# A 12-layer decoder on one core: the causal mask moves from TensorE to a fused VectorE operation, and three small steps change engine

## The chip, the core and the metric

The kernel runs on one core of a Trainium2 chip. The metric is the device time of one execution in microseconds. Before the change it is 2720.16 us (median of three runs, 2719.19 to 2727.39).

## What is computed

The reference is a post-norm decoder of twelve layers, four rounds of self-mixing, cross-attention and feed-forward, each as `x = layernorm(x + layer(x))`, on `x` of 4 x 512 x 128 (batches, positions, width) with a context of 4 x 154 x 128. Four of the layers bear on this case.

```python
# L0_xattn: cross-attention whose result goes through a residual and a norm of its own
# L1_ffn (8 heads of 64, gated experts) and L2_attn (16 heads of 64, keys = values): causal
sim  = einsum('bhid,bhjd->bhij', q * scale, k)
sim  = where(causal_mask, very_negative, sim)
attn = softmax(sim, axis=-1)
out  = einsum('bhij,bhjk->bhik', attn, values)
# L2_xattn: cross-attention with biases on q, k, v
q = einsum('bsd,ed->bse', query, Wq) + bq
```

## The kernel before, in words

Everything stays on chip between layers. The program gives each engine one list of instructions in the order in which the Python code issues them; a tile framework adds the semaphore waits. So the order of the code is the order on every engine's queue, and an engine that waits holds up all that stands behind it on its own queue. Layers overlap at their seams: an outer loop calls the generators of two layers in turn, after patterns written by hand (`ORDER`, `BESIDE`), and during one layer it also issues weight loads and `send` calls for the next.

**The causal layers.** A unit is two heads (one per half of the partitions) of one batch: 16 units in `l1_ffn`, 32 in `l2_attn`. The class `Causal` cuts a unit's score triangle into three parts, A, B and C (`PARTS`): A is query tile 3 with 512 keys, B is query tile 2 with 384 keys and tile 0 with 128, C is tile 1 with 256. Each part has the two heads in the two banks of one PSUM tile `scc`. For each part:

- `scores` (L1124): matmuls q x k into `scc` (L1131), and then a bf16 matmul of the identity with a 128 x 128 triangle of -2^100 or 0, `cmaskb`, that accumulates the mask onto the diagonal block (L1137), two per query tile: 8 per unit.
- `maxima` (L1147): one VectorE reduction per query tile for both heads, PSUM to `nm`, with the sign turned (L1149): 4 per unit.
- `exps` (L1151): ScalarE exp of the score plus `nm`, PSUM to `pr`, with the row sum in `zs` (L1155): 8 per unit.
- `norm` (L1160): VectorE reciprocal of `zs` (L1161), GpSimd multiplies `pr` by it (L1164).
- `turned` (L1170): TensorE transposes of `pr` into PSUM `ptc` (L1180), copied to `pT`; `products` (L1188): matmuls with the values into `avc` (L1193).

In `l2_attn.step` (L1506) part A's copy to `pT` is on VectorE (L1516), B's on ScalarE (L1527), C's on VectorE (L1541). The step handles unit i+1's scores beside unit i's transposes and products, and makes unit i+2's queries and keys (`psqk`, L1465; `q` on VectorE L1469, `k` on ScalarE L1470) and values (`psv`, L1475; L1478). Its output projection is `ypo` (L1486). All these PSUM tiles share three places of two banks each, so a matmul that opens a tile waits until the tile that had the place was read. `l1_ffn.step` (L1352) has the same three parts among more TensorE work (`psve` L1283, `psg` L1305, `yT` L1326) and more VectorE work (`vtmp` L1288, `gT` L1310).

**send** (L396) prepares queries or keys of the next attention: a projection in PSUM, ScalarE adds the bias and scales (`raw`, L408; a bias scaled first on VectorE, L406), GpSimd splits `raw` in three bf16 parts (L409 to L412), and SP writes them out. Queries are 512 columns wide, keys 154. Seven of the eight sends of L2_xattn fall into the L2_attn stage.

**L0_xattn** is `cross_attention` with `shuffled=True`: 16 units of four heads. A step (L1037) has two halves, each with two score tiles, two VectorE reductions to `top` (L963) and exps. Between the halves `link_maxima` (L493) brings the maxima of the next unit into the queries: TensorE transposes `pmx` (L499), then a VectorE add to `qP` (L501). At the end of a step GpSimd splits the maxima in four small operations (L488 to L491). In `more_sums` (L996) a unit's result is transposed on VectorE (`ot`, L1012), a reciprocal is taken (L1014), and GpSimd multiplies (`zt`, L1015). After the last unit of a batch `inner` adds the residual on GpSimd and takes statistics on VectorE; `outer` (L1029) subtracts the mean and scales, four operations by `applied` on GpSimd (L346), then three GpSimd operations with gamma, beta and the residual (L1031 to L1033).

Of the kernel before, what the change touches and what calls it, by code (L numbers as in the profile page):

```python
# [11 lines left out]
F32 = mybir.dt.float32  # L12
BF16 = mybir.dt.bfloat16
U8 = mybir.dt.uint8
I32 = mybir.dt.int32
AF = mybir.ActivationFunctionType
ALU = mybir.AluOpType
AX = mybir.AxisListType
# [3 lines left out]
P = 128  # L22
B, S, D = 4, 512, 128
NT = S // P
H, DK = 16, 8
KC = 154
# [3 lines left out]
MASKED = -float(2**100)  # L30
# [144 lines left out]
def decoder_kernel(ctx: ExitStack, tc: tile.TileContext, x, ctxT, mask1, mask3, packs, offsets, out, layers):  # L175
# [168 lines left out]
    def applied(dst, ys, n, mv, rs, on=nc.vector):  # L344
        for t in range(n):
            on.tensor_scalar(  # L346
                dst[:, t, :], ys[:, t, :], mv[:, t, 0:1], rs[:, t : t + 1], ALU.subtract, ALU.mult
            )
# [44 lines left out]
    Q_ROWS, K_ROWS = ((1, 1, 3), (6, 1, 2), (0, 1, 1)), ((0, 3, 3), (1, 6, 2), (2, 1, 1))  # L393
    SLOT = 32

    def send(far, order, w, rhs, scale, bias, raw, part, on=nc.gpsimd, by=nc.sync):  # L396

        n = rhs.shape[-1]
        pj = psum_t("ps_proj", kind="a" if "a" in ring else "t")
        nc.tensor.matmul(pj[:, :n], lhsT=w, rhs=rhs, start=True, stop=True)  # L400
        if bias is None:
            nc.scalar.activation(raw, pj[:, :n], AF.Copy, scale=scale)
        else:
            if scale != 1.0:
                scaled_bias = small.tile([P, 1], F32, tag="sb", name="sb", bufs=2)
                nc.vector.tensor_scalar(scaled_bias, bias, scale, None, ALU.mult)  # L406
                bias = scaled_bias
            nc.scalar.activation(raw, pj[:, :n], AF.Identity, bias=bias, scale=scale)  # L408
        on.tensor_copy(part[:, 0, :], raw)  # L409
        on.tensor_tensor(raw, raw, part[:, 0, :], ALU.subtract)  # L410
        on.tensor_copy(part[:, 1, :], raw)
        on.tensor_tensor(part[:, 2, :], raw, part[:, 1, :], ALU.subtract)  # L412
        for i, (at, gap, m) in enumerate(order):
            for r in range(2):
                rows = far[r].rearrange("(s k) p c -> (k p) s c", k=DK)
                by.dma_start(
                    rows[:, at : at + gap * (m - 1) + 1 : gap, :],
                    part[64 * r : 64 * r + 64, i : i + 1, :].to_broadcast([64, m, n]),
                )
# [7 lines left out]
    def sends(i, x_T):  # L427

        name, w = layers[i], weights[layers[i]]
        if name.endswith("xattn"):  # L430
            scale = 1.0 if name == "L0_xattn" else DK ** -0.5

            def key(b):
                return lambda room: send(
                    far_kc[b], K_ROWS, w["wk"], ctx_sb[:, b, :], 1.0, w.get("bk"), *room(KC)
                )

            def query(b):
                return lambda room: send(
                    far_q[i % 2][b], Q_ROWS, w["wq"], x_T[:, b, :], scale, w.get("bq"), *room(S)  # L440
                )

            return [x for b in range(B) for x in ((-1, ("k", b), key(b)), (b, ("q", b), query(b)))]
        if name == "L3_attn":
            xd = []

            def down(room):
                xd.append(room("xd"))
                pd = psum_t("xd", kind="a" if "a" in ring else "t")
                nc.tensor.matmul(pd, lhsT=w["wd"], rhs=x_T[:, 0, :], start=True, stop=True)  # L450
                evacuate(xd[0], pd)

            scale = DK ** -0.25
            return [
                (0, "down", down),
                (0, ("q", 0), lambda room: send(far_q[i % 2][0], Q_ROWS, w["wq"], xd[0], scale, None, *room(S))),
                (0, ("k", 0), lambda room: send(far_k[0], K_ROWS, w["wk"], xd[0], scale, None, *room(S))),
            ]
        return []
# [356 lines left out]
    def cross_attention(w, cur, new, last, room, scale, mask=None, shuffled=False):  # L816
# [179 lines left out]
        def more_sums(n):  # L996
            b, j = divmod(n, 4)
            m = made[b]
            av = m["av"]
            nc.tensor.matmul(  # L1000
                av, lhsT=m["v2"][:, j].rearrange("p g k -> p (g k)"), rhs=weights_of.pop((n, 4)),
                start=False, stop=True, skip_group_check=True,
            )
            if not shuffled:
                avs = copied(av, keep)
                agenda.add(n + 2, [lambda: divided(avs, m["o"], j)])
                if j == 3:
                    agenda.add(n + 3, out_pieces(b, m["o"], w, keep, cur, new, last, split=True))
                return

            ot = keep.tile([P, 16, 32], F32, tag="ot", name="ot", bufs=2)
            nc.vector.transpose(ot.rearrange("p s k -> p (s k)"), av.rearrange("p (q s) -> p s q", s=16))  # L1012
            rec = small.tile([P, 16], F32, tag="recx", name="recx")
            nc.vector.reciprocal(rec, ot[:, :, DK])  # L1014
            nc.gpsimd.tensor_tensor(  # L1015
                m["zt"][:, j, :].rearrange("p (s d) -> p s d", d=DK), ot[:, :, :DK],
                rec[:, :, None].to_broadcast([P, 16, DK]), ALU.mult,
            )
            if j == 3:
                zt = m["zt"]  # L1020
                xs = cur["x"][:, b * NT : (b + 1) * NT, :]
                ys = keep.tile([P, NT, D], F32, tag="ys", name="ys")
                stats = []

                def inner():
                    nc.gpsimd.tensor_tensor(zt, zt, xs, ALU.add)
                    stats.extend(ln_stats(zt, NT, "i"))

                def outer():  # L1029
                    applied(ys, zt, NT, *stats, on=nc.gpsimd)  # L1030
                    nc.gpsimd.tensor_tensor(ys, ys, w["gamma"][:, None, :].to_broadcast([P, NT, D]), ALU.mult)  # L1031
                    nc.gpsimd.tensor_tensor(ys, ys, w["beta"][:, None, :].to_broadcast([P, NT, D]), ALU.add)
                    nc.gpsimd.tensor_tensor(ys, ys, xs, ALU.add)  # L1033

                agenda.add(n + 2, [inner, outer] + finish_pieces(b, ys, new, last, split=True))
# [72 lines left out]
    class Causal:  # L1108
# [6 lines left out]

        def __init__(self, pool, room):
            self.ap, self.room, self.work = pool, room, None
            self.mask = pool.tile([P, P], BF16, name="cmaskb", bufs=1)
            make_causal_mask(nc, self.mask, MASKED)
            self.nm = {}  # L1120
            self.pr = {}
            self.pT = {}

        def scores(self, u, part, q, k):  # L1124

            sc = psum2("scc")
            for i, (qt, at) in enumerate(self.PARTS[part]):
                n = (qt + 1) * P
                for r in range(2):
                    rows = slice(64 * r, 64 * r + 64)  # L1130
                    nc.tensor.matmul(  # L1131
                        sc[:, r, at : at + n], lhsT=q[rows, qt * P : n], rhs=k[rows, :n], start=(i == 0), stop=False,
                        skip_group_check=True,
                    )
            for qt, at in self.PARTS[part]:
                for r in range(2):
                    nc.tensor.matmul(  # L1137
                        sc[:, r, at + qt * P : at + (qt + 1) * P], lhsT=identb, rhs=self.mask, start=False, stop=True,
                        skip_group_check=True,
                    )  # L1140
            nt = len(self.PARTS[part])
# [3 lines left out]
            self.pr[u, part] = pr  # L1145

            def maxima():  # L1147
                for i, (qt, at) in enumerate(self.PARTS[part]):
                    nc.vector.tensor_reduce(nm[:, i, :], sc[:, :, at : at + (qt + 1) * P], AX.X, ALU.max, negate=True)  # L1149

            def exps():  # L1151
                for i, (qt, at) in enumerate(self.PARTS[part]):
                    to = at + (qt + 1) * P
                    for r in range(2):
                        nc.scalar.activation(  # L1155
                            pr[:, r, at:to], sc[:, r, at:to], AF.Exp, bias=nm[:, i, r : r + 1],
                            accum_out=zs[:, i, r : r + 1],
                        )

# [39 lines left out]
    def l1_ffn(w, cur, new, last, room):  # L1199
# [19 lines left out]
        def gate(b):  # L1219
# [20 lines left out]

            def split():
                rest = gm.rearrange("p (t c r) e -> p t c (r e)", t=NT, c=NC)
                left = pool.tile([P, NT, NC, 2 * NE], F32, tag="left", name="left", bufs=1)
                for i in range(3):
                    part = pb[:, :, :, i, :]
                    nc.gpsimd.tensor_copy(part, rest)
                    if i < 2:
                        nc.gpsimd.tensor_tensor(left, rest, part, ALU.subtract)
                        rest = left
# [1156 lines left out]
```

## Time and profile before

| | |
|---|---|
| profiled execution, own time | 2720.02 us |
| its span on the core | 2718.2 us |
| median of the runs | 2720.16 us |
| granted TensorE clock, mean | 0.954 |
| busy share TensorE, VectorE, ScalarE, GpSimd | 90%, 62%, 46%, 39% |
| L0_xattn, 4 x 4 units | about 249 to 393 us |
| L1_ffn | about 985 to 1440 us |
| L2_attn | about 1446 to 1860 us |
| mask matmuls L1137 | 384 |
| reductions L1149 | 192, 820 ns mean |
| reciprocal and multiply of L0_xattn, L1014 and L1015 | 16 each, 253 and 406 ns |

How to read what follows. A row of a timeline is start (us), duration (us), engine, line, operation, output <- inputs, shapes, and after `x` how many instructions in a row are merged; in brackets the idle time before it and what ended it. A row of the chain of waits is start, length and what the chain passes through; the chain is followed back from the last instruction of the program, so what lies on it sets the end. TensorE rows are pipelined: the start of the next row tells more than the end of one. PEld is TensorE's weight load.

### The profile page before, as it was taken

To read this page: it belongs to the slowest core of one execution; us is meant where nothing else is said; L and a number is where in the kernel's file an instruction comes from. 1 tells how busy PE (TensorE), PEld (TensorE's weight loads), DVE (VectorE), ACT (ScalarE), POOL (GpSimd) and SP (SyncE) were. 2 spreads that over 40 slices of the span, in tenths; PEclk is the share of its full clock that TensorE was granted. 3 is DMA by queue.
4 is the path that set the end of the run, shared out by engine and by line. 5 is a ranking of instruction groups with operands and counts; after the bars stand their busy time and mean duration, and the time that the engine had idled before them with its cause. 6 is when DMAs were issued, how large, how long until landed. Compare 5 with 4: busy or idle time off the path is not lost. (4 is left out here: it accounts for less than half of the span.)

```text
span 2718.2 us, 38015 instructions
## 1 busy us (share of the span) xinstructions
PE 2445.7 (90%) x14378; PEld 1179.3 (43%) x14378; DVE 1681.6 (62%) x2872; ACT 1251.3 (46%) x2533; POOL 1071.5 (39%) x1406
## 2 busy tenths in 40 slices
PE   5898789988877989999999999998988999899998
PEld 1233234433333444444444555554455233445665
DVE  6796741188997665555445555556755887664444
ACT  3775432377652433333233555553543777343221
POOL 2342540157675326555452444443355342320000
PEclk7998989989989999999999999998997899899999
DMA  5421310000002400000000000002102240410000
GB/s 153 116 79 57 100 35 0 1 0 1 0 16 75 146 7 1 1 1 1 1 1 1 15 10 3 12 13 72 49 1 59 71 120 20 132 33 1 5 5 8
DMA packets 75559, 96.40 MB, mean 35 GB/s; under 512 B 23664, under 2 KB 62320, under 8 KB 75376
## 3 DMA queue, kind: packets, MB, share of 16 engines
q1 hardware_dynamic: 74224, 92.14, 11.7%
q8 instruction: 113, 1.85, 0.3%
q10 hardware_dynamic: 1152, 1.84, 0.2%
q14 instruction: 70, 0.57, 0.1%
HBM read 63.92 MB, written 33.49 MB: 36 GB/s over the span
## 5 line engine op out<-in xcount | busy, mean ns | idle before, releaser
L1164 POOL TENSOR_TENSOR pr<-pr,zs 128x1024 f32<-128x1024 f32 x192 | 237.1, 1252 | 234.2 <-DVE zs L1161 185.4
L670 DVE TENSOR_REDUCE top<-sc 128x2 f32<-128x1024 f32 x256 | 300.8, 1215 | 46.1 <-PE sc L666 43.2
L691 ACT ACTIVATE pT<-st 128x512 f32<-128x512 f32 x512 | 276.2, 598 | 88.2 <-PE st L682 85.1
L1155 ACT ACTIVATE pr<-scc,nm 128x256 f32<-128x256 f32 (+3 forms) x384 | 198.2, 526 | 173.2 <-DVE nm L1149 107.7
L1149 DVE TENSOR_REDUCE nm<-scc 128x2 f32<-128x1024 f32 x192 | 153.5, 820 | 167.5 <-PE scc L1137 166.3
L963 DVE TENSOR_REDUCE top<-scx 128x4 f32<-128x616 f32 x256 | 191.4, 791 | 90.1 <-PE scx L950 79.2
L969 ACT ACTIVATE pTx<-stx 128x512 f32<-128x512 f32 x256 | 139.1, 596 | 213.4 <-PE scx L950 128.2
L2137 POOL TENSOR_TENSOR hh<-hh,cs 128x1024 f32<-128x1024 f32 x64 | 149.3, 2354 | 74.5 <-DVE hh L2133 50.2
L1288 DVE TENSOR_TENSOR vtmp<-psve,gm 128x1024 f32<-128x1024 f32 x64 | 78.3, 1224 | 153.7 <-PE psve L1283 58.4
L705 PE MATMUL av<-pT,vbuf 128*32 128x256 f32 x2048 | 162.8, 393 | 8.6 <-ACT avs L505 8.6
L337 POOL TENSOR_TENSOR rsf<-mvf,eps 128x4 f32<-128x4 f32 x48 | 9.8, 204 | 394.3 <-DVE mvf L335 393.3
L488 POOL CAST nmP<-top 128x16 bf16<-128x16 f32 x96 | 25.3, 264 | 344.4 <-DVE top L963 180.3
L1131 PE MATMUL scc<-k,q 64*128 64x512 f32 (+3 forms) x768 | 143.9, 472 | 6.5 <-ACT pr L1155 2.7
L1180 PE MATMUL ptc<-ident,pr 128*128 128x128 f32 x960 | 137.8, 281 | 10.5 <-POOL pr L1164 8.9
L2133 DVE TENSOR_TENSOR_SCAN hh<-da,pb 128x1024 f32<-128x1024 f32 x64 | 142.6, 2269 | 0.0
L1293 POOL TENSOR_TENSOR vtmp<-vtmp 128x512 f32<-128x512 f32 x60 | 76.1, 1269 | 162.3 <-DVE vtmp L1288 137.7
L666 PE MATMUL sc<-kP,qP 64*128 64x512 bf16 x512 | 106.0, 412 | 33.9 <-DVE top L670 16.6
L1283 PE MATMUL psve<-w_L_ffn,xT 128*128 128x512 f32 x256 | 123.1, 605 | 14.5 <-ACT pr L1155 11.2
L2146 PE MATMUL acc<-hh,ident 128*128 128x512 f32 x256 | 132.9, 646 | 3.1 <-DVE yt L2155 1.9
L1193 PE MATMUL avc<-pT,v 128*64 128x512 f32 (+3 forms) x768 | 131.4, 449 | 0.5 <-DVE pT L1516 0.5
L1180 PEld LDWEIGHTS ptc<-ident,pr 128*128 128x128 f32 x960 | 103.1, 141 | 50.5 <-issue 26.4
L1326 PE MATMUL yT<-gT,w_L_ffn 128*128 128x512 f32 x256 | 123.4, 605 | 0.0
(417 smaller groups left out, 5065.1 us busy)
## 6 DMA issues: line engine op xcount, KB each, us to landing
qP<-far_q SPq DMA_DIRECT2D x24, 768.0 KB, 5.8
w_L_ffn<-in_L_ffn SPq DMA_DIRECT2D x24, 512.0 KB, 6.2
far_q<-part SPq DMA_DIRECT2D x44, 192.0 KB, 2.8
qP<-far_q SPq DMA_DIRECT2D x24, 256.0 KB, 4.2
far_q<-part SPq DMA_DIRECT2D x44, 128.0 KB, 2.4
kP<-far_k SPq DMA_DIRECT2D x7, 768.0 KB, 5.1
kP<-far_kc SPq DMA_DIRECT2D x16, 231.0 KB, 4.6
w_L_attn<-in_L_attn SPq DMA_DIRECT2D x6, 512.0 KB, 6.5
```

The costliest lines, as they stand in the source:

```text
L670: return lambda: nc.vector.tensor_reduce(top[:, qt, 2 * gp : 2 * gp + 2], sc, AX.X, ALU.max, negate=True)
L691: nc.scalar.activation(pT, st, AF.Exp)
L705: nc.tensor.matmul(m["av"][32 * g : 32 * g + 32, part], lhsT=m["v"][:, kt, 4 * j + g, :], rhs=weights_of[s, g][:, part], start=(kt == 0 an ...
L963: nc.vector.tensor_reduce(ops.maxima(a)[:, 2 * qp : 2 * qp + 2, 2 * gp : 2 * gp + 2].rearrange("p i r -> p r i"), sc, AX.X, ALU.max, negat ...
L969: nc.scalar.activation(pT, st, AF.Exp)
L1131: nc.tensor.matmul(sc[:, r, at : at + n], lhsT=q[rows, qt * P : n], rhs=k[rows, :n], start=(i == 0), stop=False, skip_group_check=True,)
L1149: nc.vector.tensor_reduce(nm[:, i, :], sc[:, :, at : at + (qt + 1) * P], AX.X, ALU.max, negate=True)
L1155: nc.scalar.activation(pr[:, r, at:to], sc[:, r, at:to], AF.Exp, bias=nm[:, i, r : r + 1], accum_out=zs[:, i, r : r + 1],)
L1164: nc.gpsimd.tensor_tensor(pr[:, :, at : at + n], pr[:, :, at : at + n], zs[:, i, :, None].to_broadcast([P, 2, n]), ALU.mult)
L1180: nc.tensor.transpose(pt[:, r, to : to + P], self.pr[u, p][:, r, lo : lo + P], ident)
L2133: nc.vector.tensor_tensor_scan(flat, das[g % 2][:, c].rearrange("p n t -> p (n t)"), pbs[c].rearrange("p n t -> p (n t)"), 0.0, ALU.mult, ...
L2137: nc.gpsimd.tensor_tensor(m["h", j][c], m["h", j][c], m["C", j], ALU.mult)
```

## The change

Four edits, and one in memory that goes with them.

1. In the causal layers the mask matmuls go. The mask tile grows to 128 x 512 (zeros, then the triangle) and `maxima` becomes one fused VectorE operation per query tile and head, in place on PSUM: `out = (score + mask) * -1`, with the running minimum, started at 3e38, into `nm`. `exps` takes its input with scale -1. In the built program each fused operation is two instructions, the operation and a read of its accumulator into `nm` (one column), and every fused operation but a part's first waits for the accumulator read before it.
2. The multiply by the reciprocal in L0_xattn (`zt`) is on VectorE.
3. `applied` in `outer` of L0_xattn is on VectorE.
4. In the sends of L2_xattn bias and scale are one VectorE operation, (psum + bias) * scale; the scaled bias of before is not computed.
5. `left` in `l1_ffn` takes the buffer of `sig`, which has had its last use.

```diff
-    def send(far, order, w, rhs, scale, bias, raw, part, on=nc.gpsimd, by=nc.sync):
+    def send(far, order, w, rhs, scale, bias, raw, part, on=nc.gpsimd, by=nc.sync, biased=nc.scalar):
...
         if bias is None:
             nc.scalar.activation(raw, pj[:, :n], AF.Copy, scale=scale)
+        elif biased == nc.vector:
+            nc.vector.tensor_scalar(raw, pj[:, :n], bias, scale, ALU.add, ALU.mult)
         else:
...
+            biased = nc.vector if name == "L2_xattn" else nc.scalar
...
             nc.vector.reciprocal(rec, ot[:, :, DK])
-            nc.gpsimd.tensor_tensor(
+            nc.vector.tensor_tensor(
                 m["zt"][:, j, :].rearrange("p (s d) -> p s d", d=DK), ot[:, :, :DK],
...
-                    applied(ys, zt, NT, *stats, on=nc.gpsimd)
+                    applied(ys, zt, NT, *stats)
...
-            self.mask = pool.tile([P, P], BF16, name="cmaskb", bufs=1)
-            make_causal_mask(nc, self.mask, MASKED)
+            self.mask = pool.tile([P, S], BF16, name="cmaskb", bufs=1)
+            nc.gpsimd.memset(self.mask[:, : S - P], 0.0)
+            make_causal_mask(nc, self.mask[:, S - P :], MASKED)
...
-                        sc[:, r, at : at + n], lhsT=q[rows, qt * P : n], rhs=k[rows, :n], start=(i == 0), stop=False,
-                        skip_group_check=True,
-                    )
-            for qt, at in self.PARTS[part]:
-                for r in range(2):
-                    nc.tensor.matmul(
-                        sc[:, r, at + qt * P : at + (qt + 1) * P], lhsT=identb, rhs=self.mask, start=False, stop=True,
+                        sc[:, r, at : at + n], lhsT=q[rows, qt * P : n], rhs=k[rows, :n], start=(i == 0), stop=True,
                         skip_group_check=True,
                     )
...
                 for i, (qt, at) in enumerate(self.PARTS[part]):
-                    nc.vector.tensor_reduce(nm[:, i, :], sc[:, :, at : at + (qt + 1) * P], AX.X, ALU.max, negate=True)
+                    n = (qt + 1) * P
+                    for r in range(2):
+                        of = sc[:, r, at : at + n]
+                        nc.vector.tensor_tensor_reduce(
+                            of, of, self.mask[:, S - n :], -1.0, 3.0e38, ALU.add, ALU.min, nm[:, i, r : r + 1]
+                        )
...
-                            pr[:, r, at:to], sc[:, r, at:to], AF.Exp, bias=nm[:, i, r : r + 1],
+                            pr[:, r, at:to], sc[:, r, at:to], AF.Exp, bias=nm[:, i, r : r + 1], scale=-1.0,
...
-                left = pool.tile([P, NT, NC, 2 * NE], F32, tag="left", name="left", bufs=1)
+                left = pool.tile([P, NT, NC, 2 * NE], F32, tag="sig", name="left", bufs=1)
```

More of the change, by code (lines that the diff above doesn't have):

```diff
@@ L431, in sends @@
             scale = 1.0 if name == "L0_xattn" else DK ** -0.5
+            biased = nc.vector if name == "L2_xattn" else nc.scalar
             def key(b):
                 return lambda room: send(
-                    far_kc[b], K_ROWS, w["wk"], ctx_sb[:, b, :], 1.0, w.get("bk"), *room(KC)
+                    far_kc[b], K_ROWS, w["wk"], ctx_sb[:, b, :], 1.0, w.get("bk"), *room(KC), biased=biased
                 )
@@ L439, in query @@
                 return lambda room: send(
-                    far_q[i % 2][b], Q_ROWS, w["wq"], x_T[:, b, :], scale, w.get("bq"), *room(S)
+                    far_q[i % 2][b], Q_ROWS, w["wq"], x_T[:, b, :], scale, w.get("bq"), *room(S), biased=biased
                 )
```

## The prediction

> **What bounds the kernel now.** The page says TensorE, 90% busy, but that is a mean over stages. So I first cut the span in windows, then followed the chain of waits and the timelines inside each stage that is edited.
>
> ```profile
> 1150.00:1250.00 100.00, 97.53 (x396) 43.84 (x394) 53.52 (x74) 34.78 (x83) 55.47 (x65) 1.00 0.00 1
> 1550.00:1650.00 100.00, 97.11 (x614) 54.32 (x614) 57.01 (x102) 51.85 (x155) 43.88 (x39) 1.00 0.04 9
> ```
>
> Columns: window, length, busy us of TensorE, its weight loads, VectorE, ScalarE, GpSimd, then the clock. L1_ffn (first row) and L2_attn have TensorE 97% busy at full clock and VectorE little over half. In L1_ffn TensorE is the bound: its rows follow one another, and a mask takes a place in that row:
>
> ```profile
> 1106.64 0.39 PE L1131 MATMUL scc<-k,q 64*128 64x128 f32 x4
> 1106.96 0.40 PE L1137 MATMUL scc<-cmaskb,identb 128*128 128x128 bf16 x4
> 1107.29 0.60 PE L1305 MATMUL psg<-gateT,pick 64*128 64x512 bf16 x2
> ```
>
> In L2_attn it is not so simple. The chain through one 12.00 us unit:
>
> ```profile
> 1645.14 1.72 PE psqk L1465 x4
> 1646.86 1.07 PE scc L1131 x8
> 1647.92 0.34 PE scc L1137 x4
> ...
> 1648.29 1.29 DVE nm L1149 x2
> 1649.58 0.09 DVE zs L1161
> ...
> 1650.17 1.45 ACT pr L1155 x7
> 1651.62 0.91 ACT pT L1527
> ...
> 1652.58 0.66 PE ptc L1180 x4
> ```
>
> From the end of part B's scores (1648.27) the chain leaves TensorE for 4.31 us: reductions, exps, the copy of `pT` that frees the PSUM place of part C's transposes. TensorE works beside it (transposes B, `avc`, `ypo`, scores C, `psv`), and is done at almost the same moment. Two loops of equal length: shortening TensorE's gains nothing if the other grows.
>
> In L0_xattn neither engine is full (TensorE 84 and 74%, VectorE 83 and 77% of the windows 260 to 280 and 280 to 300 us). The timelines of VectorE and GpSimd show who waits:
>
> ```profile
> 290.08 0.25 DVE L1014 RECIPROCAL recx<-ot 128x16 f32<-128x16 f32 x1
> 290.25 1.44 DVE L963 TENSOR_REDUCE top<-scx 128x4 f32<-128x616 f32 x2
> 292.71 0.69 DVE L501 TENSOR_TENSOR qP<-qP,pmx 128x1024 bf16<-128x1024 bf16 x1 [1.02 <-PE pmx L499]
> ```
> ```profile
> 290.42 0.40 POOL L1015 TENSOR_TENSOR zt<-ot,recx 128x128 f32<-128x128 f32 x1 [3.81 <-DVE recx L1014]
> 290.76 0.25 POOL L488 CAST nmP<-top 128x16 bf16<-128x16 f32 x1
> ```
>
> GpSimd idles 3.81 us before `zt`, yet the split behind it needs only the reductions that ended at 289.43. The in-order queue holds it 1.3 us; TensorE (0.89 idle before `pmx`) and VectorE (1.02) wait in turn.
>
> **Part 1, masks.** Gone from TensorE: 8 matmuls per unit. By the starts of their successors they take 0.33 + 0.21 + 0.21 = 0.75 us in an L1_ffn unit; by streaming alone (a pair 0.107, from the closest starts, 0.12 at 1651.80) 0.43, if a change of data type is what the rest is and stays. L1_ffn has 16 units: 7 to 12 us, I take 10. Its VectorE has room: 53%, and below some 1.8 us more of 25.
>
> The cover for that in L1_ffn: part B's maxima end 0.9 us later, but the exps stand behind a `pT` copy on ScalarE that ends 1.3 us after the reductions did. The later `gT` is used one piece (6 us) later.
>
> Added on VectorE: no row of before is this operation. Its length by the tensor_tensor rows on PSUM and SBUF (128 columns 0.29, 512: 0.691, 1024: 1.22, between them 384: 0.56 and 256: 0.43). The accumulator read: nearest a reciprocal of two columns, 0.15 long, begun 0.08 before its predecessor ends; and a waiting successor starts 0.04 after (the statistics rows). So each pair costs 0.11 more than its operation. Bounds: 0.02 (the read hidden like any short successor) and 0.24 (ScalarE's accumulator read, 0.20, plus the wait). I take 0.11, as it comes from VectorE's own rows. Part A: 2 x 0.80 = 1.60 against 1.22; part B: 2 x 0.67 + 2 x 0.40 = 2.14 against 1.29; C: 2 x 0.53 = 1.06 against 0.69. In sum 4.8, where the reductions, by the starts of their successors, took 3.0.
>
> [...] The only running operation in the trace, the scan at L2133, takes 2.27 us for 1024 columns, twice the 1.22 of an in-place tensor_tensor on PSUM (L2130). By the scan's row part B would be 3.2. [...]
>
> L2_attn, plain unit: 12.00 - 0.22 - 0.34 (masks A and B, on the chain) + 0.85 - 0.09 (the exps no longer wait for the reciprocal, by the built program's waits) = 12.2. With masks at streaming cost, 0.32, it is 12.4; I take 12.3. TensorE alone would need 11.4: it now waits 0.9 for part B. The part A loop holds: scores A to scores B leave TensorE 3.32 us of work, maxima 1.60 + exps 1.34 + gaps 0.2 = 3.1. Behind maxima A stand the copy of `pT` (L1516) and `q`; transposes A end 1.6 us after scores A too, so the copy is not late. Some 21 plain units x 0.3 = +6. Three units a stage also hold a norm (L346 x4, 2.22 us) in front of maxima A, where +0.4 for C and +0.4 for A show: +2.5.
>
> **Part 4, sends.** In the seven units with a send the chain runs through GpSimd:
>
> ```profile
> 1624.34 0.90 ACT pT L1527
> 1625.24 0.60 ACT raw L408
> ...
> 1629.65 3.00 POOL pr L1164 x3
> ```
>
> `raw` stands behind exps B and the `pT` copy. On VectorE it is queued before maxima C, in a gap of 2.5 us: projection done about 2.9 us after scores B, `raw` by 3.6, GpSimd free of `pr` A at 4.2. A query's four GpSimd steps then end at 7.9 instead of 8.7, and no masks precede: 15.3 falls to about 14.3, three times. A key's end at 5.9, so the unit is the plain 12.3 instead of 13.0, four times. Together -6. Maxima C wait behind `raw` only if the projection is over 1 us late; then part C's exps, not on the chain. SP's six writes per send follow earlier; nothing is moved past them.
>
> L2_attn in sum: 6 + 2.5 - 6 = +3, rounded up to +4. Ends: overhead 0.02 gives -0.09 x 4 x 25 = -9, so -5; 0.24 gives +13, so +17.
>
> **Parts 2 and 3, L0_xattn.** `zt` leaves GpSimd: the split starts at 289.45, `pmx` when TensorE is free (291.17), `qP` as soon as VectorE is. VectorE gains 1.02 of idle and pays 0.32 (L894, the same shape, 0.29, and the wait for the reciprocal): 0.7 per unit, nine units with that row: -6. `applied` takes 3.13 us from GpSimd and adds 1.11 to VectorE (L346 there, at 350). Before, GpSimd's chain `ys` held the split, and `qP` idled 6.97, 3.26 and 2.79 us in three units. Redrawn, `qP` comes about 4, 2 and 2 earlier: -8. Two residual adds also start earlier: -1. Sum -15. Behind both operations on VectorE stand the next reductions.
>
> Against it: at 1126.13 a VectorE operation with two SBUF inputs (L1100) took 1.20 instead of 0.42 beside a GpSimd operation, and L346 2.22 instead of 1.11. `zt` and `applied` are of these two kinds. 16 x 0.25 for `zt` (a split step's length) and 3 x 1.2 is 7.6. A loss is excluded: 1.02 of idle is more than 0.32 + 0.25. Between -7 and -15 I take -11. The stages behind begin earlier by as much: TensorE is at 92% only from 380 on.
>
> Edit 5 and the second memset (0.20 us for 128 columns before, so some 0.5 for 384): nothing; GpSimd idles half of both stages, and `left` is last read three units before `sig` is written. Uncovered they would cost under 1 us once.
>
> **Sum.** -11 - 10 + 4 = -17. The profiled execution's own time is 2720.02, as good as the median: 2703.
>
> **The rivals.**
> - *The gain goes into the chain.* Accumulator pairs near 0.24, L0_xattn at -7, L1_ffn at -10: +17 - 17 = 0: 2720. For it: L2_attn's two loops are equal now. Against: it takes a ScalarE row for a VectorE cost.
> - *The fused operation is slow, and the kernel slower.* Place: maxima A and B in L2_attn. It decides from 0.28 us of overhead a pair: 4 + (0.28 - 0.11) x 4 x 25 = 21, the other two gains. At the scan's rate: B +1.07, A +1.07, of which 0.2 fits: +1.9 a unit, 30 units, 2703 + 57 = 2760. For it: it is the one accumulating row in the trace. [...]
> - [...] `applied` and `zt` blocked throughout, L1_ffn's masks at 7: -2 - 7 + 4: 2715, no change.
>
> **Chances.** Forecast 0.58 (its own range 2688 to 2711), first rival 0.15, second 0.17, third 0.10. A run can tell 0.3%, 8 us, from no change: faster 0.58, same 0.25, slower 0.17. Low end: -15 - 12 - 5 - 3 for the odd seam = 2685. High end: into the second rival at 0.30 a pair, 19 for part B and, past its 0.2 of room, some 5 for part A: 2727, say 2728; what is above holds about 0.12.
>
> **What would show it.** Right: L1_ffn's unit 25 to 24.3 us; L2_attn's plain units (starts of L1516) 12.2 to 12.4 with the chain still through `nm`, `pr` and `pT` L1527, and TensorE waiting before `psv`; the fused operation 0.69 at 512 columns; the 15.28 us units near 14.3; the `qP` rows' 1.02 gone. Wrong: fused rows near 1.2 at 512; L2_attn units under 12 (the read is free) or over 12.8; L346 in L0_xattn at 2 us; a `ptc` that waits for GpSimd in plain units.

## The result and the profile after

The changed kernel takes 2703.76 us (median of 4 runs, 2701.47 to 2705.39), the kernel before beside it 2719.68: a ratio of 0.9934, with a 95% interval of 0.9917 to 0.9951. The profiled execution took 2705.39, with a span of 2703.4.

Stage lengths in the profiled executions, measured the same way in every kernel below: L0_xattn from the first `scx` matmul to the first `psh` of L0_ffn, so with its seam; L1_ffn from the first `psqk` to the last `psve`; L2_attn from the first `psqk` to the last `ypo`.

| us | before | after | difference | forecast |
|---|---|---|---|---|
| L0_xattn and seam | 133.2 | 123.2 | -10.0 | -11 |
| L1_ffn | 419.0 | 411.5 | -7.5 | -10 |
| L2_attn | 417.8 | 420.6 | +2.8 | +4 |
| span | 2718.2 | 2703.4 | -14.8 | -17 |

The sum of the three is -14.7. The first `scx` starts 1.5 later (in L0_attn, which is not edited), and stages behind give back about as much.

The windows of L1_ffn and L2_attn: length, busy us of TensorE, weight loads, VectorE, ScalarE, GpSimd, clock.

```profile
1150.00:1250.00 100.00, 95.74 (x375) 42.74 (x374) 58.13 (x121) 33.50 (x85) 54.19 (x60) 0.98 0.00 1
1550.00:1650.00 100.00, 92.64 (x542) 50.47 (x539) 66.40 (x194) 49.31 (x151) 43.26 (x38) 1.00 0.04 9
```

TensorE's 97 became 96 and 93, VectorE's 54 and 57 became 58 and 66. Work has moved to VectorE, and TensorE now stands still where it worked on masks. TensorE's waits say for whom, over L1_ffn before, over L1_ffn after and over L2_attn after (us in total, times, longest):

```profile
PE psve L1283 <- ACT pr L1155: 11.2, 9, 1.6
```
```profile
PE psve L1289 <- ACT pr L1161: 11.9, 9, 2.2
PE psve L1289 <- DVE gT L1316: 3.8, 4, 1.8
```
```profile
PE psv L1481 <- ACT pr L1161: 13.0, 23, 1.6
PE ptc L1186 <- ACT pT L1533: 5.7, 23, 0.2
```

The chain through one plain unit of L2_attn after, to be held against the chain of before:

```profile
1620.09 1.09 PE scc L1137 x8
...
1621.32 0.57 DVE scc L1153
1621.88 0.07 DVE nm L1153
...
1621.97 0.57 DVE scc L1153
...
1623.38 0.04 DVE zs L1167
...
1623.48 0.24 ACT pr L1161
...
1623.95 1.45 ACT pr L1161 x7
1625.41 0.91 ACT pT L1533
...
1626.37 0.66 PE ptc L1186 x4
```

It is the same chain. Both mask steps have left it, and part B's maxima take 2.06 us (1621.32 to 1623.38) where they took 1.29. The plain units are 12.21 to 12.33 long. TensorE now waits twice in each, before `psv` for the place that exps B hold and before part C's `ptc` for the copy of `pT`:

```profile
1625.46 0.66 PE L1481 MATMUL psv<-ident,k 128*128 128x128 f32 x4 [0.55 <-ACT pr L1161]
1626.37 0.66 PE L1186 MATMUL ptc<-ident,pr 128*128 128x128 f32 x4 [0.25 <-ACT pT L1533]
```

In L0_xattn, VectorE and then GpSimd:

```profile
290.12 0.29 DVE L1019 TENSOR_TENSOR zt<-ot,recx 128x128 f32<-128x128 f32 x1
290.32 1.50 DVE L967 TENSOR_REDUCE top<-scx 128x4 f32<-128x616 f32 x2
291.74 0.68 DVE L505 TENSOR_TENSOR qP<-qP,pmx 128x1024 bf16<-128x1024 bf16 x1
```
```profile
289.24 0.26 POOL L492 CAST nmP<-top 128x16 bf16<-128x16 f32 x1 [3.37 <-DVE top L967]
```

The split starts with its reductions' end, as foreseen, and `qP` has lost its wait of 1.02 us.

### The profile page after: what moved, and what is told of

The parts are those of the page before. It is cut to its first block, busy times and chain, and to the rows that moved or that the text cites. A ratio compares the mean times of both kernels' runs of the same rounds, so it can differ in the third digit from the quotient of the medians.

```text
span 2703.4 us, 37772 instructions
## 1 busy us (share of the span) xinstructions
PE 2410.7 (89%) x13974; PEld 1161.6 (43%) x13994; DVE 1754.2 (65%) x3484; ACT 1247.0 (46%) x2525; POOL 1056.1 (39%) x1376
## 4 chain that ended last, share of the span: by engine, by line
PE 62%; DVE 16%; ACT 9%; POOL 5%; issue 4%; DMA 2%; SPq 1%; POOLq 0%; DVEq 0%; ACTq 0%
PE psgu L1935 4%; PE psve L1289 4%; PE av L709 4%; PE yT L1332 3%; PE scc L1137 3%; PE ype L1946 3%; ACT pr L1161 3%; PE psh L1624 3%; DVE scc L1153 3%; PE avc L1199 3%; PE ptc L1186 3%; DVE top L967 2%; PE sc L670 2%; PE avx L995 2%; DVE top L674 2%
## 5 line engine op out<-in xcount | busy, mean ns | idle before, releaser
L1153 DVE CUSTOM_DVE_ANT_0 scc<-scc,cmaskb 128x256 f32<-128x256 f32 (+3 forms) x384 | 191.5, 499 | 131.4 <-PE scc L1137 112.6
L1294 DVE TENSOR_TENSOR vtmp<-psve,gm 128x1024 f32<-128x1024 f32 x64 | 78.3, 1224 | 133.2 <-PE psve L1289 133.1
```

The source lines that it names most:

```text
L1153: nc.vector.tensor_tensor_reduce(of, of, self.mask[:, S - n :], -1.0, 3.0e38, ALU.add, ALU.min, nm[:, i, r : r + 1])
```

## The experiments

The theory on trial is the prediction's: the three terms are separate, `zt`'s place in GpSimd's queue holds L0_xattn, and in L2_attn part B's maxima are on the chain while A's and C's lie beside it. Rivals: the stages give gains back to one another, or it is the sum of VectorE's work that counts. Every ratio is against runs of the kernel before on the same chip.

### One part at a time

Parts 2 and 3 alone (`e_norm_only`), the fused operation alone (`e_masks_only`), the sends alone (`e_sends_only`), each put into the kernel before.

> The kernel before with parts 2 and 3 alone (zt and applied of L0_xattn on VectorE). Theory (the split of the maxima was held by GpSimd's queue): the 1.02 us before qP in the plain units goes, qP's interval falls from 5.39 to 4.66 us, L0_xattn ends 10 us earlier, all later stages keep their length: 2710. Rival (the stages behind give it back, because TensorE is at 92% from 380 us on): nothing left at the end, 2718 to 2720.

Measured: 2706.27 us, ratio 0.9952 (0.9939 to 0.9964). L0_xattn 123.4, so -9.8; L1_ffn 418.2 and L2_attn 417.9 as before. `qP`'s plain interval (from one start to the next) is 4.66. The stages behind keep the gain; the other 3 us of the median lie in stages that this edit does not touch.

> The kernel before with the fused operation alone, in both causal layers. Theory: L1_ffn 7.5 us shorter; L2_attn's plain units 12.00 to 12.3 (21 of them, +6), the norm units +2.5, the units with a send unchanged or up to 0.3 longer: L2_attn +8 to +10. In sum 0 to +2: 2720 to 2722. Rival (the sends gained nothing in the changed kernel, and the fused operation costs L2_attn only the 2.7 us seen there): 2715.

Measured: 2723.74 us, ratio 1.0015 (1.0008 to 1.0022): alone, the fused operation makes the kernel slower. L1_ffn 411.2 (-7.8), but L2_attn 432.1: +14.3, half as much again as expected, with 1.5 of it from half clock (see the last section). Plain units are 12.22 to 12.35 as with the change; units with a send grow too: 13.46 for 13.01, 15.83 to 16.05 for 15.28.

> The kernel before with the biases of the sends on VectorE alone. Theory: in L2_attn the three 15.28 us units fall to about 14.5 and the four 13.02 us units to about 12.4, plain units stay at 12.00: L2_attn -5, in sum 2714 to 2715. Rival (the shorter send units of the changed kernel come from the masks that left TensorE): send units within 0.2 of before, 2719 to 2720.

Measured: 2710.23 us, ratio 0.9962 (0.9949 to 0.9974). L2_attn 410.8 (-7.0): units of 14.16 and 12.44, plain units 12.00. Of the 7.0, 1.5 is one stretch at half clock that the trace of before has and this one has not. The other few us of the median lie in stages that this edit does not touch.

So in L2_attn the sends gain 7.0 with the old masks and 11.5 with the fused ones (432.1 to 420.6). Without the stretches at half clock it is some 5.5 and 8.5, and the seven units with a send alone give 5.7 and 8.1: these two terms are not separate. With a send on ScalarE, `raw` stands behind exps B and the copy of `pT`, and both end later when the maxima are slower: the first query's `raw` starts 5.6 us behind the start of scores B before, and 6.2 in `e_masks_only`. On VectorE it starts 4.5 behind with the old masks (`e_sends_only`) and 4.3 with the change.

### The changed kernel without the fused operation in L2_attn

```diff
-        causal = Causal(pool, room)
+        causal = Causal(pool, room, fused=())      # l2_attn; (0, 1, 2) in l1_ffn
...
+                    if part not in self.fused:
+                        nc.vector.tensor_reduce(nm[:, i, :], sc[:, :, at : at + n], AX.X, ALU.max, negate=True)
+                        continue
```

with the mask matmuls for the parts that are not fused.

> The changed kernel, but L2_attn keeps its mask matmuls and reductions (fused operation in L1_ffn alone). Theory (the fused operation loses in L2_attn, where part B's maxima are on the chain, and gains in L1_ffn): L1_ffn as in the changed kernel, plain units of L2_attn back at 12.00, send units as short as or shorter than with the change (14.3 and 12.4): L2_attn -5 against before, in sum 8 us under the changed kernel: 2696. Rival (fused operation neutral in L2_attn, its +2.7 from something else): 2702 to 2705.

Measured: 2687.92 us, ratio 0.9884 (0.9869 to 0.9900). L2_attn 412.5, plain units 12.00, sends 14.16 and 12.44. The theory holds: in L2_attn the operation, as it was put in, loses 8.1. The kernel gains more on the changed one than the 8 expected, 14 us by the ratios: L1_ffn, whose code is the same, has 408.4 here and 411.5 there, which is half clock again.

### Which part's maxima are on the chain

Only part B not fused (`e_l2_b_old`: A and C fused), then only part B fused (`e_l2_b_alone`).

> The changed kernel, but in L2_attn part B keeps its mask matmuls and its reductions; A and C are fused. Theory (part B's maxima stand on the chain, those of A and C beside it): the chain of a plain unit loses 0.85 and gets 0.34 back, TensorE's own work is 11.4 + 0.34: plain units 11.75, TensorE's wait before psv gone, L2_attn some 13 us shorter than in the changed kernel: 2691. Rival (it is the sum of VectorE's work that counts, 0.85 of its 1.8 us per unit taken away): plain units 12.1 to 12.2, 2699 to 2701.

Measured: 2687.75 us, ratio 0.9897 (0.9883 to 0.9912). Plain units 11.78 to 11.81; L2_attn 411.0, so 9.6 shorter than with the change, where some 13 were expected. TensorE's row, which had 0.55 of idle with the change, has none:

```profile
1620.73 0.70 PE L1137 MATMUL scc<-k,q 64*128 64x256 f32 x4
1621.36 0.66 PE L1490 MATMUL psv<-ident,k 128*128 128x128 f32 x4
```

> The changed kernel, but in L2_attn only part B is fused; A and C keep mask matmuls and reductions. Theory (B on the chain): the chain keeps B's 0.85 and gets A's mask (0.22) back: plain units 12.4 to 12.5, L2_attn 3 to 6 us longer than in the changed kernel: 2707 to 2710. Rival (the sum of VectorE's work counts, 0.9 of its 1.8 us taken away): plain units 12.1, 2699 to 2701.

Measured: 2703.56 us, ratio 0.9956 (0.9943 to 0.9968); plain units 12.43 to 12.53, L2_attn 423.4. Two halves of the same edit, one 0.5 us a unit shorter than the change and one 0.2 longer. The sum of VectorE's work would have made both shorter: that rival falls.

### The copy ahead of the exps

```diff
-                expB()
             if T_:
                 tB = causal.turned(i, 1)
                 nc.scalar.copy(*tB)
+            if S_:
+                expB()
```

> The changed kernel, but in L2_attn ScalarE copies pT of part B ahead of exps B and not behind them: exps B wait for the maxima anyway, which end about 0.2 us after this copy could. Theory (chain from the maxima through exps B and this copy to part C's transposes): the 0.25 us before ptc goes, the 0.55 before psv stays, since psv needs the place that exps B free: plain units 12.0, L2_attn -6 to -7, 2697. Rival (all of the 0.8 us that TensorE waits per unit hangs on the copy): plain units 11.5, 2683. Other rival (the copy is late and delays exps B): 12.3 or longer, 2704 or more.

Measured: 2689.89 us, ratio 0.9902 (0.9888 to 0.9917). Plain units 11.62 and 11.86, between theory and rival. TensorE's rows:

```profile
1618.34 0.66 PE L1481 MATMUL psv<-ident,k 128*128 128x128 f32 x4 [0.55 <-ACT pr L1161]
1618.83 0.60 PE L1186 MATMUL ptc<-ident,pr 128*128 128x128 f32 x4
```

The waits did as the theory said: 0.55 stays, 0.25 is gone. But the unit fell by 0.47 to 0.6. `ptc` starts 0.49 behind `psv`; with the change it started 0.91 behind. The wait so cost 0.42 and not 0.25: idle time is counted from the end of `psv`'s row, and without a wait the next row starts 0.17 before that end. The other 0.05 to 0.18 of the unit stays open.

### Queue or engine

`zt` is on GpSimd again, but issued behind `split_maxima` (`e_zt_late`); and `zt` alone moved to VectorE in the kernel before (`e_zt_only`).

> The changed kernel, but zt is on GpSimd again, queued behind the split of the maxima and not ahead of it. Theory (what held L0_xattn was zt's place in GpSimd's queue, not the engine it ran on): the wait before qP stays gone, and VectorE is rid of 0.3 us of zt per unit: qP's interval 4.35 to 4.66 us, L0_xattn 0 to 3 us shorter than in the changed kernel: 2701 to 2704. [...]

Measured: 2699.92 us, ratio 0.9938 (0.9924 to 0.9951). `qP`'s interval is 4.44 and L0_xattn 123.9, against 123.2 with the change (the eight traces with the change's L0_xattn lie between 122.2 and 126.4). Its place in the queue was the matter, not the engine.

> The kernel before with part 2 alone (zt of L0_xattn on VectorE, applied stays on GpSimd). Theory (nine plain units gain 0.7 us each by zt, the rest comes from applied leaving GpSimd's chain): qP's plain interval 4.66 us, the waits of 6.97, 3.26 and 2.79 us stay within 1 us, L0_xattn 5 to 7 us shorter of the 10. Rival (applied does nothing: once zt is gone the split comes in time everywhere): the whole 10.

Measured: 2710.88 us (one run); L0_xattn 124.2: 9.0 of the 10, more than the theory's 5 to 7 and near the rival. `qP`'s plain interval is 4.66, as foreseen, and the three long waits fell by 1.0 to 1.7. `applied` still on GpSimd does hold `qP` in one unit, but that costs little in the end:

```profile
309.64 0.69 DVE L501 TENSOR_TENSOR qP<-qP,pmx 128x1024 bf16<-128x1024 bf16 x1 [5.94 <-PE pmx L499]
```

With `applied` on VectorE as well this wait is 0.39 and the interval before it falls from 11.70 to 8.94. Three later intervals then grow (6.44 to 7.30, 7.83 to 8.37, 6.60 to 7.31) and give back 2.1 of the 2.8. So `applied` is worth about 1, though between single traces of this stage 1 us is within the scatter.

### Where the fused operation puts its result

With the change the operation writes back onto `scc`. Here it writes into `pr` in SBUF, and the exps work in place on `pr` (`e_sb`); then with the copy first as well (`e_sb_copy_first`).

```diff
-                            of, of, self.mask[:, S - n :], -1.0, 3.0e38, ALU.add, ALU.min, nm[:, i, r : r + 1]
+                            pr[:, r, at : at + n], of, self.mask[:, S - n :], -1.0, 3.0e38, ALU.add, ALU.min,
+                            nm[:, i, r : r + 1]
...
-                            pr[:, r, at:to], sc[:, r, at:to], AF.Exp, ...
+                            pr[:, r, at:to], pr[:, r, at:to], AF.Exp, ...
```

> The changed kernel, but the fused operation writes its result into pr in SBUF (the exps then work in place on pr) and not back onto scc in PSUM. The built program then has no wait between one fused operation and the next, and psv waits for VectorE's maxima and not for exps B. Theory (the 0.55 us before psv is the wait for the PSUM place that exps B hold; 0.09 us a pair is a wait of the operation for its predecessor on the same tile): pairs 0.57 to 0.60 apart at 384 columns (0.66 with the change), the wait before psv gone, but ptc C still waits for the copy of pT that stands behind exps B: plain units 12.0 to 12.1, 2697. Rival (the 0.66 is the operation's own length, and TensorE's wait moves whole to ptc C): 12.3 again, 2704. Other rival (with its result in SBUF the operation is blocked by GpSimd): rows over 0.8 at 384 columns, 2710 or more.

> The same, and in L2_attn ScalarE copies pT of part B ahead of exps B. Theory (both waits of TensorE then have no cause left, and TensorE alone sets the unit): plain units 11.3 to 11.5, L2_attn 24 us shorter than with the change and 13 shorter than with the copy alone: 2677 to 2680. Rival (GpSimd's multiplication of pr or VectorE becomes the bound, since the result goes to SBUF): plain units 11.9 or longer, 2690.

Measured: 2648.50 us, ratio 0.9734 (0.9717 to 0.9751); with the copy first 2644.21, ratio 0.9716 (0.9701 to 0.9731), which the intervals don't tell apart from the former. Both are faster than either kernel, and `e_sb` by much more than any of its three theories said: L1_ffn 386.8 us (411.5 with the change), L2_attn 391.2 (420.6), plain units 11.24 to 11.26. The copy first, from which its theory expected a gain of its own, adds nothing: the plain units are the same, since in `e_sb` TensorE's rows already follow one another without a stop. So 11.25 is TensorE's own time, which the prediction put at 11.4. The rows that had the two waits:

```profile
1582.94 0.66 PE L1481 MATMUL psv<-ident,k 128*128 128x128 f32 x4
1583.43 0.60 PE L1186 MATMUL ptc<-ident,pr 128*128 128x128 f32 x4
```

VectorE's and ScalarE's rows in a plain unit of `e_sb`:

```profile
1590.65 0.56 DVE L1153 CUSTOM_DVE_ANT_0 pr<-scc,cmaskb 128x384 f32<-128x384 f32 x1 [0.43 <-PE scc L1137]
1591.13 0.08 DVE L1153 DVE_READ_ACCUMULATOR2_ANT nm<- 128x1 f32 x1
1591.13 0.55 DVE L1153 CUSTOM_DVE_ANT_0 pr<-scc,cmaskb 128x384 f32<-128x384 f32 x1
```
```profile
1591.25 0.61 ACT L1161 ACTIVATE pr<-pr,nm 128x384 f32<-128x384 f32 x1 [0.42 <-DVE nm L1153]
```

Pairs follow each other in 0.48 us instead of 0.66. And the first exp starts 0.60 after the first pair began, when only that pair is done; with the change exps B began 2.16 after it (1621.32 to 1623.48), behind the last of the four. In the changed program every fused operation waits for its predecessor's accumulator read, and the exps wait for them all; with the result in another tile there is no wait between the operations, and the exps follow the heads one by one.

That is one difference. The other is that the PSUM place is free when VectorE has read it, and not when the exps have. `e_sb_held` takes this one back: after each part's exps ScalarE also copies one element of `scc`, so that the place stays held until then.

> The version with the fused operation's result in SBUF, but after each part's exps ScalarE copies one element of scc, so that the PSUM place is held until the exps end, as with the change; the pairs stay without a wait between them. Theory (most of what that version gains is the earlier release of the PSUM places): L1_ffn back near the changed kernel's 411.5 us, between 400 and 412; plain units of L2_attn 11.8 to 12.0 (12.3 less 0.5 for the pairs of part B, plus up to 0.2 for the added copy); 2683 to 2695. Rival (the gain is that of the pairs without a wait): L1_ffn 387 to 390, plain units 11.3 to 11.4, 2650 to 2655.

Measured: 2665.67 us, ratio 0.9807 (0.9790 to 0.9825). The two stages answer differently. L1_ffn goes back to 408.1: there the theory is right, and the gain is the place, some 18 of the 21 us (the other 3 are two stretches at half clock that `e_sb` has not). TensorE's waits over L1_ffn, in `e_sb` and in `e_sb_held`:

```profile
PE psve L1289 <- DVE nm L1153: 2.7, 3, 1.8
```
```profile
PE psve L1290 <- ACT zs L1165: 12.5, 9, 1.5
```

L2_attn stays at 389.6 with plain units of 11.24 to 11.26: there the theory falls and the rival holds: the gain is that the pairs have no wait between them and the exps follow them. What each of these two brings was not separated.

## Why the prediction was right, and where only in sum

**L2_attn's plain unit: right.** Forecast 12.3, measured 12.21 to 12.33; the fused operation took 0.70 at 512 columns and 0.66 from pair to pair at 384, so 0.09 beyond its 0.57 where 0.11 was taken. The scan's rate, the second rival, is out. That the operation would follow the tensor_tensor rows and not the scan's was the author's assumption, which no row of the trace of before showed; the result showed 0.70 at 512 columns for the 0.69 taken. The 0.09 was a wait in this program and not the price of the read, as `e_sb` shows (0.48 from pair to pair at 384). The -0.09 for the reciprocal did not come: exps B begin 0.10 after the maxima's end (1623.38 to 1623.48), and began 0.11 after it before.

**L2_attn's +4: right through two errors that cancel.** The fused operation cost +14.3 and not +8.5, the sends gained 11.5 and not 6; without the half clock it is some +12.8 and -8.5. The step that failed is the count: "Some 21 plain units x 0.3 = +6". Thirteen units of 12.0 that became 12.2 to 12.35 made some 3.7, and the norm units 3.4 where 2.5 was taken; not counted was that slower maxima also lengthen the first two units (by 1.1) and the seven with a send (by 3.7, about 0.45 for a key and 0.54 to 0.77 for a query), and that the send on VectorE would take the latter back. The query units ended at 14.29 for the 14.3 forecast, the key units at 12.65, not 12.3. That the sum met +4 is luck, and the measured +2.8 is itself 1.5 too low by the half clock that the trace of before had alone.

**L1_ffn: mechanism right, the size too at equal clock.** The term of 10 us came to 7.5 in these two traces. TensorE ran at half clock (0.50 in the third column from the end) for 6.8 us of the stage before and three times 3.4 after:

```profile
1003.30:1010.10 6.80, 5.64 (x11) 1.81 (x10) 4.15 (x15) 3.03 (x5) 1.22 (x2) 0.50 0.00 0
```
```profile
994.40:997.80 3.40, 2.91 (x4) 0.67 (x2) 2.97 (x12) 0.46 (x1) 0.64 (x2) 0.50 0.00 0
1004.60:1008.00 3.40, 3.40 (x6) 1.04 (x4) 1.98 (x9) 1.24 (x5) 2.51 (x4) 0.51 0.00 0
1178.70:1182.10 3.40, 3.40 (x6) 0.87 (x5) 0.00 (x1) 0.00 (x0) 0.00 (x0) 0.50 0.00 0
```

Traces with equal time at half clock can be compared: with 3.4 us of it the stage takes 418.2 and 418.3 with the masks (`e_norm_only`, `e_sends_only`) and 408.4 with the fused operation (`e_l1_masks`), with 6.8 us 419.0 (before) and 410.0 (`e_l2_b_old`). So the term is 9 to 10. The stretch at 1178.7 begins behind a stop of 2.25 us before `psve`, where the longest before was 1.6; four of the seven traces with this form of L1_ffn have it. "TensorE is the bound" was still not the whole of it: TensorE idled 23.6 us in the stage before (waits over 0.1 us summed), 11.2 of it before `psve` for the exps, and 28.1 after. Masks of 12 us less 4.5 of new waiting would be 7.5, not 9 to 10; that this sum does not close stays open. That the places behind those waits were worth some 18 us, the prediction did not see. Of its mask figures, the pair by streaming is 0.110 to 0.112 by the closest starts and not 0.107, which changes nothing.

**L0_xattn: -10 for -11, again by two errors that cancel.** `zt` brought 9.0, not 6: it shortens units that are not plain by as much as 1.2 (7.71 to 6.51). `applied` brought about 1, not 8: the step "Redrawn, `qP` comes about 4, 2 and 2 earlier: -8" took single waits for gains. What holds the later units instead is not settled. The third rival's price was small: 13 of the 16 rows of `zt` took 0.29 us, and the other three, of 1.36, 1.36 and 0.75, lay beside a GpSimd operation of over 1 us; `applied` had one row of 0.94 where 0.33 is usual. One of the long rows, and GpSimd's beside it:

```profile
304.05 1.36 DVE L1019 TENSOR_TENSOR zt<-ot,recx 128x128 f32<-128x128 f32 x1
```
```profile
303.98 1.27 POOL L1037 TENSOR_TENSOR ys<-ys,x 128x512 f32<-128x512 f32 x1
```

**The rivals.** "The gain goes into the chain" was there in L2_attn alone, and undone by the sends. The number of operations, 16 a unit for 4, is not what made the fused operation lose in L2_attn as first written (+14.3 alone): `e_sb` has the same 16 and gains 29 us on the changed kernel there (391.2 for 420.6). It was what each waited for.

## What to carry to other kernels

Ask of each operation not only what it costs but which tile it writes and how long that tile keeps its place: here, writing the same result to another tile brought 55 us, where the whole change brought 16. Weigh edits in the units where they meet, since two of them can be worth more together than apart. And a wait that disappears is a gain only if nothing else is due just behind it.

## What the runs showed of the hardware

Behind some stops of TensorE in the two causal layers the traces show its clock at half (0.50) for 3.4 us (for 6.8 at 1003.30 in the trace of before). In `e_masks_only`, TensorE's rows and the window behind them (the clock stands before the last two numbers):

```profile
1630.79 0.66 PE L1186 MATMUL ptc<-ident,pr 128*128 128x128 f32 x4 [2.14 <-POOL pr L1170]
1631.79 0.66 PE L1186 MATMUL ptc<-ident,pr 128*128 128x128 f32 x2 [0.34 <-POOL pr L1170]
1632.24 3.39 PE L1471 MATMUL psqk<-xT,w_L_attn 128*128 128x512 f32 x4
```
```profile
1632.00:1634.00 2.00, 2.00 (x5) 0.97 (x5) 1.23 (x1) 0.00 (x0) 0.00 (x0) 0.50 0.00 0
```

`psqk` takes 3.39 us where it takes 1.88, and the unit 13.79 where a plain one has 12.3: about 1.5 us for each such stretch. L2_attn had one before, none after and two in `e_masks_only`, so of +14.3 some 1.5 is this, and +2.8 would be +4.3 without it. Not every stop of this length has one behind it: before, the stop (1.85) ahead of 1631.70 had none (`psqk` 1.88), and the one ahead of 1731.93 (1.86) had one (`psqk` 3.04). In `e_sb` a stop of 1.09 had one, which the same stop did not have in `e_sb_copy_first` and `e_sb_held`:

```profile
1668.48 0.66 PE L1186 MATMUL ptc<-ident,pr 128*128 128x128 f32 x4 [1.09 <-POOL pr L1170]
1669.48 0.54 PE L1186 MATMUL ptc<-ident,pr 128*128 128x128 f32 x2 [0.34 <-POOL pr L1170]
1669.81 3.51 PE L1471 MATMUL psqk<-xT,w_L_attn 128*128 128x512 f32 x4
```

The stops ahead of these stretches, and of those of L1_ffn before and after, lasted 1.09 to 2.25 us; in L2_attn one short burst and another 0.34 of idle stood behind them. Why only some stops of such a length had a stretch behind them, no run showed.

Also unexpected: the same accumulator read takes 0.13 to 0.145 us in the changed kernel and 0.07 to 0.085 in `e_sb`. A waiting successor is not the reason, since the last read of a part takes 0.14 too, though the reciprocal behind it starts along with it (both at 1623.24 with the change); what is stays open.
